# Gated graph layers: 1 - z from the sigmoid of the negated sum, and the state update as three GpSimd operations per half

## Chip, cores and metric

The kernel runs on one core of a Trainium2 chip. The metric is device time in microseconds (us) of one execution. Engines: TensorE (PE; PEld is its weight load), VectorE (DVE), ScalarE (ACT), GpSimd (POOL) and SyncE (SP).

## What is computed

Two graph networks follow each other, each with a residual and a layer norm. The change is in the first, four gated layers over 16 graphs of 1024 nodes with 128 channels:

```python
h = x
for i in range(4):
    hw = einsum('bnc,cd->bnd', h, weight[i])
    m = einsum('bjn,bjd->bnd', adj, hw)
    gx = m @ w_ih[i].T + b_ih[i];  gh = h @ w_hh[i].T + b_hh[i]
    xr, xz, xn = split(gx, 3);     hr, hz, hn = split(gh, 3)
    r = sigmoid(xr + hr)
    z = sigmoid(xz + hz)
    n = tanh(xn + r * hn)
    h = (1.0 - z) * n + z * h
x = layernorm(x + h * mask)
```

The second network thins the adjacency first (a sequential rule on rows and columns, `_dilate`), and then applies three graph convolutions with batch norm. The thinning needs only the adjacency, not the first network's output.

## The kernel before

The run has two parts. In the first, the class `Gated` computes the gated layers, and `FixPoint` the thinned adjacency beside it. In the second, `Sage` computes the convolutions. The change touches only `Gated`.

`Gated` holds two graphs at a time, as two streams. The loop in `run` goes over pairs of graphs, over the 4 layers, and over the two streams: 64 calls of `layer`. The state `h` of a graph lies transposed, channels on the 128 partitions and 1024 nodes along the row, and is worked on in two halves of 512 nodes (`f` = 0, 1). A call of `layer` has these parts:

- Aggregation (L1096): 32 matmuls, 8 blocks of the adjacency for the high and the low part of the split features, for both halves. The sums go through ACT to `h_ms` (L1099).
- Gates (L1108), for each half: r from two matmuls, the hidden and the input part of n from one each, z from two; each of these matmuls shows as two records. ACT makes r (L1118), DVE two operations on n's sum (L1121, L1123), ACT the tanh (L1124, into the tile `h_r`) and z (L1127, into `h_z`).
- Update: z*h (L1131 for half 0, L1135 for half 1) on POOL, (z - 1)*n on DVE (L1136), and new h = z*h - (z - 1)*n on POOL (L1137). For half 0 the first product stands right after z; the others stand after both halves. In the very last layer of the last graph, `aid` is DVE in place of POOL.

The order on all engines (PE, DVE, ACT, POOL, SP) is the order of the program's text, by a manual schedule: each engine takes its instructions in that order, and an instruction that waits holds back all behind it on its engine. What runs beside a layer is placed by calls of `aside(n)`, at fixed points of the layer. They do two things. They advance `FixPoint.steps` by one step (a scan of 128x1024 on DVE, L739; comparisons, L870, L872, L900; Abs on ACT; short transposes on PE; one affine_select on POOL, L780; loads of `f_a` on POOL's queue, L687). And they start the other stream's next layer: `next_layer` transposes that stream's h, half 0 at point 5, half 1 at point 7 (L1041), and splits it for the aggregation (L1029, L1034).

Between graphs there is a boundary layer, on each stream: `finish` transposes h back, masks it on ACT (L1071), adds it to x on POOL (L1074) and stores the sum from POOL's queue (L1076, `e_sum`); `load_x` loads the next graph's x (L1025), `load_adj` its adjacency (L1020), both from POOL's queue too; `begin_rows` splits the new x (ACT L1060, POOL L1061), `begin` transposes it (L1053). The x tiles have three buffers, so a load of x waits for the store of the graph three before it. The gate tiles `h_r`, `h_z`, `h_zh` have two buffers each, one for each half. L1992 on DVE looks over rows of the adjacency, once in each second layer.

Of the kernel before, what the change touches and what calls it, by code (L numbers as in the profile page):

```python
# [8 lines left out]
F32 = mybir.dt.float32  # L9
# [5 lines left out]
AF = mybir.ActivationFunctionType  # L15
ALU = mybir.AluOpType
# [8 lines left out]
C = 128  # L25
NB = N // P
HF = 512
L0 = 4
# [27 lines left out]
class Dilate:  # L56
# [15 lines left out]
    def __init__(self, ctx, tc, cst, adj, not_r):  # L72
        self.tc, self.nc, self.cst, self.adj, self.not_r = tc, tc.nc, cst, adj, not_r
        nc = self.nc
        pool = lambda name, **k: ctx.enter_context(tc.tile_pool(name=name, **k))
        self.one = pool("d_one", bufs=1)
        self.two = pool("d_two", bufs=2)
        self.small = pool("d_small", bufs=3)
        self.dram = pool("d_dram", bufs=1, space=DRAM)
        self.ps = pool("d_ps", bufs=1, space=PSUM)  # L80

        self.removed = [self.dram.tile([N, N], BF, name=f"rt{b}") for b in range(B)]

        self.coef = self.one.tile([B, ROW], F32, name="coef")  # L90
        nc.vector.memset(self.coef, 1.0)
        nc.vector.memset(self.coef[:, TAIL + 1:TAIL + 2], -1.0)
        nc.vector.memset(self.coef[:, TAIL + 2:TAIL + 3], -0.5)
        nc.vector.memset(self.coef[:, TAIL + 5:TAIL + 6], 2.0)
        self.stage = self.one.tile([P, B, ROW], BF, name="stage")
        for i, v in ((1, -8.5), (2, 1.0), (3, MAGIC), (4, -MAGIC), (5, 0.0)):
            nc.vector.memset(self.stage[:, :, TAIL + i:TAIL + i + 1], v)
        self.counts = self.one.tile([P, B, NB], F32, name="counts")
        self.free = {}
# [824 lines left out]
class Gated:  # L924
# [7 lines left out]
    def __init__(self, ctx, tc, cst, x, adj, weight, w_ih, w_hh, b_ih, b_hh, summed, bad):  # L932
        self.tc, self.nc, self.cst = tc, tc.nc, cst
        self.x, self.adj, self.summed, self.bad = x, adj, summed, bad
        nc = self.nc
        pool = lambda name, **k: ctx.enter_context(tc.tile_pool(name=name, **k))
        self.adjp = pool("h_adj", bufs=NB)
        self.one = pool("h_one", bufs=1)
        self.wk = pool("h_wk", bufs=2)

        self.ps6 = pool("h_ps6", bufs=6, space=PSUM)
        self.wi = self.one.tile([C, L0, 3, C], F32, name="h_wi")
        self.wh = self.one.tile([C, L0, 3, C], F32, name="h_wh")
        self.bi = self.one.tile([C, L0 * 3], F32, name="h_bi")
        self.bh = self.one.tile([C, L0 * 3], F32, name="h_bh")
        self.bs = self.one.tile([C, L0 * 3], F32, name="h_bs")
        self.given = weight, w_ih, w_hh, b_ih, b_hh

    def bank(self):
        return self.ps6.tile([P, HF], F32, name="h_g")  # L950
# [19 lines left out]
    def prepare(self):  # L970
        nc, ident = self.nc, self.cst["ident"]
        bank = self.bank
        three = lambda p: p[:, :3 * C].rearrange("p (g c) -> p g c", g=3)
        wt = self.wk.tile([P, 4, P], F32, name="h_w")
        for l in range(L0):
            for n, dst in enumerate((self.wi, self.wh)):
                pt = bank()
                for g in range(3):
                    nc.tensor.transpose(pt[:, g * C:(g + 1) * C], self.w_in[l, n][:, g, :], ident)
                (nc.vector.tensor_copy, nc.scalar.copy)[n](dst[:, l], three(pt))  # L980
            pt = bank()
            nc.tensor.transpose(pt[:, :C], self.w[:, l, :], ident)
            nc.vector.tensor_copy(wt[:, l, :], pt[:, :C])
        for l in range(L0):
            pt = bank()
            nc.tensor.matmul(three(pt), wt[:, l, :], self.wi[:, l], start=True, stop=True)
            (nc.vector.tensor_copy, nc.scalar.copy)[l % 2](self.wi[:, l], three(pt))

        for t, dst in zip(self.b_in, (self.bi, self.bh)):
            pt = bank()  # L990
            nc.tensor.transpose(pt[:, :L0 * 3], t, ident[:L0 * 3, :L0 * 3])
            nc.vector.tensor_copy(dst, pt[:, :L0 * 3])
        nc.vector.tensor_add(self.bs, self.bi, self.bh)

    def load_test(self, n):
        if n < B * 2:
            self.test = self.wk.tile([P, N], F32, name="h_test", bufs=1)
            self.nc.sync.dma_start(self.test, self.adj[n // 2, n % 2 * P:(n % 2 + 1) * P, :])
# [79 lines left out]
    def layer(self, st, l, aside):  # L1078

        nc, wk = self.nc, self.wk  # L1080

        aid = nc.vector if (st.b, l) == (B - 1, L0 - 1) else nc.gpsimd
        half = [slice(f * HF, (f + 1) * HF) for f in range(2)]
        bank = self.bank
        pm = [bank() for f in range(2)]
        ms = []
        for f in range(2):
            for n, part in enumerate((st.hi, st.lo)):
                if (f, n) != (0, 1):
                    aside(2 * f + n)  # L1090
                if l == 0 and f == 1 and n == 0:
                    st.begin(1)
                for j in range(NB):
                    if (f, n, j) == (0, 1, NB // 2):
                        aside(1)
                    nc.tensor.matmul(pm[f], part[:, j, :], st.adj[j][:, half[f]],  # L1096
                                     start=(j == 0 and n == 0), stop=(j == NB - 1 and n == 1))
            m = wk.tile([C, HF], F32, name="h_ms")
            nc.scalar.copy(m, pm[f])  # L1099
            ms.append(m)  # L1100
        aside(4)
        bias = lambda t, g: t[:, 3 * l + g:3 * l + g + 1]
        w = lambda t, g: t[:, l, g, :]

        def gate(*mm):
            pg = bank()
            for i, (lhs, rhs) in enumerate(mm):
                nc.tensor.matmul(pg, lhs, rhs, start=(i == 0), stop=(i == len(mm) - 1))  # L1108
            return pg

        rest = []
        for f in range(2):
            h, m = st.ht[:, half[f]], ms[f]
            r = wk.tile([C, HF], F32, name="h_r")
            z = wk.tile([C, HF], F32, name="h_z")
            zh = wk.tile([C, HF], F32, name="h_zh")
            pr = gate((w(self.wh, 0), h), (w(self.wi, 0), m))
            nc.scalar.activation(r, pr, AF.Sigmoid, bias=bias(self.bs, 0))  # L1118
            aside(5 + 2 * f)
            ph = gate((w(self.wh, 2), h))  # L1120
            nc.vector.scalar_tensor_tensor(r, ph, bias(self.bh, 2), r, op0=ALU.add, op1=ALU.mult)  # L1121
            px = gate((w(self.wi, 2), m))
            nc.vector.tensor_add(r, px, r)  # L1123
            nc.scalar.activation(r, r, AF.Tanh, bias=bias(self.bi, 2))  # L1124
            aside("rest" if f == 0 else 8)
            pz = gate((w(self.wh, 1), h), (w(self.wi, 1), m))
            nc.scalar.activation(z, pz, AF.Sigmoid, bias=bias(self.bs, 1))  # L1127

            rest.append((r, z, zh, h))
            if f == 0:  # L1130
                aid.tensor_tensor(zh, z, h, ALU.mult)  # L1131
                aside(6)
        for f, (r, z, zh, h) in enumerate(rest):
            if f == 1:
                aid.tensor_tensor(zh, z, h, ALU.mult)  # L1135
            nc.vector.scalar_tensor_tensor(r, z, 1.0, r, op0=ALU.subtract, op1=ALU.mult)  # L1136
            aid.tensor_tensor(h, zh, r, ALU.subtract)  # L1137
        aside(9)

    def run(self, steps):  # L1140
# [937 lines left out]
```

## Time and profile before

| | us |
|---|---|
| Runs | 2232.93, 2233.61, 2242.04; median 2233.61 |
| Profiled execution, its own time | 2232.83 |
| Its span in the profile | 2230.8 |
| Busy: PE, DVE, ACT, POOL | 2129.7, 1926.9, 1327.2, 1082.6 |
| Gated stage, first to last aggregation (L1096) | 34.0 to 1292.4 |
| Last gate matmul (L1108) | 1303.4 |

All times in the profile are from the start of the span. A row of the timeline gives the start, the length, the engine, the line, the operation, the tile written and those read with their shapes, and in brackets the idle time before and what ended it. A row of the groups gives the count, the busy time, the mean length in ns and the idle time before these instructions. Ends of matmuls are modelled, so the busy share of PE is to be read with the distances between its starts.

### The profile page before, as it was taken

The page shows a single profiled execution, that of the slowest core. Times are in us where ns is not written, and L with a number is a line of the kernel's source. Part 1 is how long each engine was busy: PE and PEld are TensorE (multiplying, and loading weights), DVE is VectorE, ACT ScalarE, POOL GpSimd, SP SyncE. Part 2 cuts the span into 40 slices and gives each one's busy share as a digit, 9 for nine tenths or more (in the row PEclk, how much of TensorE's full clock was granted, in tenths as well). Part 3 has the DMA queues.
Part 4 walks back from the last instruction along what each step waited for, and adds up shares of the span by engine and source line. Part 5 has one row for each costly group of instructions (what it writes and reads, how often), then busy time and mean ns, then how long its engine had stood idle before and what let it go on. Part 6 is the DMA issues. An engine that isn't in the chain of part 4 may idle for free. (4 is left out here: it accounts for less than half of the span.)

```text
span 2230.8 us, 33341 instructions
## 1 busy us (share of the span) xinstructions
PE 2129.7 (95%) x10665; PEld 1456.6 (65%) x10665; DVE 1926.9 (86%) x4338; ACT 1327.2 (59%) x3238; POOL 1082.6 (49%) x1092
## 2 busy tenths in 40 slices
PE   6999999999999999999999979999999899998987
PEld 4566655666656666555665557777777678887865
DVE  4999999999998999999999978888888766666877
ACT  3657557565565656556566465666666455556756
POOL 4347437356355364364463346777777344551002
PEclk9999999999999999999999989999999999999989
DMA  8247347347356265364383259888888577765404
GB/s 251 71 103 240 80 114 229 71 120 214 86 156 177 73 200 138 90 201 118 73 264 85 64 184 329 305 305 297 305 301 304 169 259 260 257 221 174 152 29 144
DMA packets 214396, 402.46 MB, mean 180 GB/s; under 512 B 59586, under 2 KB 80740, under 8 KB 214212
## 3 DMA queue, kind: packets, MB, share of 16 engines
q1 hardware_dynamic: 168388, 280.68, 37.3%
q0 software_dynamic: 41472, 117.46, 19.3%
q10 hardware_dynamic: 4352, 2.11, 0.4%
q8 instruction: 86, 1.41, 0.3%
q14 instruction: 98, 0.80, 0.1%
HBM read 324.49 MB, written 109.25 MB: 194 GB/s over the span
## 5 line engine op out<-in xcount | busy, mean ns | idle before, releaser
L1108 PE MATMUL h_g<-h_h,h_wh 128*128 128x512 f32 x768 | 399.2, 601 | 3.1 <-DVE h_r L1121 3.1
L1108 PE MATMUL h_g<-h_ms,h_wi 128*128 128x512 f32 x768 | 392.1, 592 | 0.0
L739 DVE TENSOR_TENSOR_SCAN f_rank<-f_a,f_first,f_pd 128x1024 f16<-128x1024 bf16 x128 | 299.2, 2343 | 3.3
L1137 POOL TENSOR_TENSOR h_h<-h_zh,h_r 128x512 f32<-128x512 f32 x126 | 205.3, 1629 | 195.2 <-DVE h_r L1136 172.2
L1096 PE MATMUL h_g<-h_a,h_hi 128*128 128x512 f32 x1024 | 282.8, 417 | 2.2 <-DMA h_a<-in_adj_dram 2.0
L1108 PEld LDWEIGHTS h_g<-h_ms,h_wi 128*128 128x128 f32 x768 | 145.6, 190 | 183.9 <-issue 166.8
L1096 PE MATMUL h_g<-h_a,h_lo 128*128 128x512 f32 x1024 | 264.1, 395 | 0.0
L1513 POOL CAST p_b<-p_at 128x512 uint8<-128x512 f32 x256 | 219.4, 879 | 84.2 <-DVE p_at L1505 59.8
L1096 PEld LDWEIGHTS h_g<-h_a,h_hi 128*128 128x128 f32 x1024 | 188.4, 188 | 63.8 <-issue 20.1
L1096 PEld LDWEIGHTS h_g<-h_a,h_lo 128*128 128x128 f32 x1024 | 190.0, 188 | 39.4
L1406 ACT ACTIVATE s_junk<-s_o 128x128 bf16<-128x128 f32 x384 | 114.0, 298 | 170.7 <-DVE s_o L1399 170.7
L1131 POOL TENSOR_TENSOR h_zh<-h_z,h_h 128x512 f32<-128x512 f32 x63 | 80.1, 1271 | 275.5 <-ACT h_z L1127 275.5
L1108 PEld LDWEIGHTS h_g<-h_h,h_wh 128*128 128x128 f32 x768 | 129.2, 190 | 85.9 <-issue 65.5
L1099 ACT COPY h_ms<-h_g 128x512 f32<-128x512 f32 x128 | 73.8, 577 | 183.3 <-PE h_g L1096 139.3
L1124 ACT ACTIVATE h_r<-h_r,h_bi 128x512 f32<-128x512 f32 x128 | 92.3, 721 | 131.2 <-DVE h_r L1123 131.1
L916 ACT ACTIVATE f_u<-f_rank,f_q 128x128 f16<-128x128 f16 (+7 forms) x128 | 110.6, 867 | 74.9 <-DVE f_rank L856 74.9
L1992 DVE SCALAR_TENSOR_TENSOR p_junk<-p_a 128x1024 bf16<-128x1024 f32 x96 | 125.7, 1309 | 0.0
L893 ACT ACTIVATE f_pd<-f_rank,f_q 128x128 f32<-128x128 f16 x128 | 59.1, 461 | 109.8 <-DVE f_q L701 106.6
L1781 PE MATMUL q_ob<-s_wxp,q_xt 128*128 128x256 f32 x512 | 123.4, 385 | 0.3
L1505 DVE SCALAR_TENSOR_TENSOR p_at<-p_nr,p_u 128x128 fp32r<-128x128 bf16 (+1 forms) x192 | 102.5, 543 | 20.5 <-ACT p_at L1497 15.0
L1492 PE MATMUL p_u<-ident_b,p_nr 128*128 128x128 bf16 x1024 | 97.2, 224 | 7.2 <-DVE p_at L1505 5.0
L1423 POOL TENSOR_TENSOR q_rl<-s_r,q_rh 128x512 fp32r<-128x512 f32 x32 | 41.1, 1285 | 128.0 <-ACT q_rh L1422 105.5
(260 smaller groups left out, 4946.3 us busy)
## 6 DMA issues: line engine op xcount, KB each, us to landing
h_a<-in_adj_dram POOLq DMA_DIRECT2D x128, 512.0 KB, 9.5
p_a<-in_adj_dram SPq DMA_DIRECT2D x96, 512.0 KB
f_a<-in_adj_dram POOLq DMA_DIRECT2D x128, 256.0 KB, 6.6
e_nr<-f_nr SPq DMA_DIRECT2D x128, 256.0 KB
p_nr<-e_nr SPq DMA_DIRECT2D x32, 1024.0 KB
h_test<-in_adj_dram SPq DMA_DIRECT2D x32, 512.0 KB
s_at<-p_b SPq DMA_DIRECT2D x32, 512.0 KB
s_ag<-s_ag SPq DMA_DIRECT2D x64, 256.0 KB
```

Of the source, the lines that this page charges most:

```text
L739: nc.vector.tensor_tensor_scan(out, a, other[:, 0, 0:1].to_broadcast([P, N]), start, op0=ALU.add, op1=ALU.bypass)
L916: nc.scalar.activation(u[:, :n1], rank[:, g, :n1], AF.Abs, bias=q[:, 1, g:g + 1], scale=q[:, 0, g:g + 1])
L1096: nc.tensor.matmul(pm[f], part[:, j, :], st.adj[j][:, half[f]], start=(j == 0 and n == 0), stop=(j == NB - 1 and n == 1))
L1108: nc.tensor.matmul(pg, lhs, rhs, start=(i == 0), stop=(i == len(mm) - 1))
L1124: nc.scalar.activation(r, r, AF.Tanh, bias=bias(self.bi, 2))
L1137: aid.tensor_tensor(h, zh, r, ALU.subtract)
L1406: self.nc.scalar.activation(junk, o[:, i, :], AF.Square, accum_out=ss[:, i:i + 1])
L1492: nc.tensor.matmul(pu[:, i * P:(i + 1) * P], v[:, 4 * f + i, j * P:(j + 1) * P], self.cst["ident_b"], start=True, stop=True)
L1505: self.nc.vector.scalar_tensor_tensor(g["at"][:, j, c0:c0 + low], v[:, j, c0:c0 + low], 0.0, pu[:, :low], op0=ALU.is_lt, op1=ALU.is_lt)
L1513: self.nc.gpsimd.tensor_copy(g["b", f][:, j, :], g["at"][:, j, f * HF:(f + 1) * HF].bitcast(F32))
L1781: nc.tensor.matmul(pb[:, i], g["xt"][:, f, blk], self.wxp, start=(i % 2 == 0), stop=False)
L1992: nc.vector.scalar_tensor_tensor(junk, a, 0.0, a, op0=ALU.is_gt, op1=ALU.not_equal, accum_out=bad[:, c:c + 1])
```

## The change

The bias of z's sigmoid is negated once (`h_bn`), and the sigmoid gets scale -1 with it, so the tile `h_z` holds 1 - z. The update is h + (1 - z)*(n - h): a subtraction, a product and a sum, all three on `aid`, that is on POOL except in the last layer. They follow z's sigmoid directly in each half. The product z*h, the DVE operation and the loop after both halves are gone.

```diff
@@ __init__ and prepare
+        self.bn = self.one.tile([C, L0 * 3], F32, name="h_bn")
...
         nc.vector.tensor_add(self.bs, self.bi, self.bh)
+        nc.vector.tensor_scalar(self.bn, self.bs, -1.0, None, op0=ALU.mult)
@@ layer
-        rest = []
         for f in range(2):
             h, m = st.ht[:, half[f]], ms[f]
             r = wk.tile([C, HF], F32, name="h_r")
             z = wk.tile([C, HF], F32, name="h_z")
-            zh = wk.tile([C, HF], F32, name="h_zh")
+            d = wk.tile([C, HF], F32, name="h_zh")
...
             pz = gate((w(self.wh, 1), h), (w(self.wi, 1), m))
-            nc.scalar.activation(z, pz, AF.Sigmoid, bias=bias(self.bs, 1))
-
-            rest.append((r, z, zh, h))
+            nc.scalar.activation(z, pz, AF.Sigmoid, bias=bias(self.bn, 1), scale=-1.0)
+            aid.tensor_tensor(d, r, h, ALU.subtract)
+            aid.tensor_tensor(d, z, d, ALU.mult)
+            aid.tensor_tensor(h, h, d, ALU.add)
             if f == 0:
-                aid.tensor_tensor(zh, z, h, ALU.mult)
                 aside(6)
-        for f, (r, z, zh, h) in enumerate(rest):
-            if f == 1:
-                aid.tensor_tensor(zh, z, h, ALU.mult)
-            nc.vector.scalar_tensor_tensor(r, z, 1.0, r, op0=ALU.subtract, op1=ALU.mult)
-            aid.tensor_tensor(h, zh, r, ALU.subtract)
         aside(9)
```

The order of the instructions in the two built programs, compared engine by engine: PE and SP have the same instructions in the same order. ACT differs in the operand of 128 sigmoids. DVE loses the two L1136 of each of 63 layers and gains the one for `h_bn`. POOL goes from 1760 to 1886 instructions, all 126 of them from the update.

The prediction calls the three new operations d, m and a, with the number of the half: d0 is n - h of half 0, m0 the product, a0 the sum; and those of before zh0, zh1 (z*h), stt0, stt1 (L1136), and h0, h1 (L1137).

## Prediction

> **What bounds the kernel now.** Only the first stage (the gated layers, with the dilation steps woven in) is edited, so I first cut the run into stretches, with the busy time of each engine. Columns: stretch, length, then busy us (and instructions) of PE, PE's weight loads, VectorE (DVE), ScalarE (ACT), GpSimd (POOL), granted clock, DMA share, GB/s.
>
> ```profile
> 59.00:1304.00 1245.00, 1238.55 (x4942) 751.46 (x4940) 1173.14 (x2360) 745.16 (x1390) 601.21 (x599) 1.00 0.47 135
> 1304.00:1318.00 14.00, 4.28 (x29) 3.31 (x29) 12.23 (x51) 6.95 (x18) 1.64 (x4) 0.66 1.04 388
> ```
>
> In the 1245 us of layers PE is idle for 6.45 us; DVE is at 94%, POOL at 48%. A busy PE need not be a PE at its rate, so I looked at starts in the timeline: the eight aggregation matmuls of 611.00 are followed by the next eight at 612.83 (229 ns each), and the gate matmuls of L1108, twelve a layer and each two records, follow each other at 0.86 us. Per layer that is 32 x 0.229 + 24 x 0.43 = 17.6 us, plus 8 transposes at 0.11 and some 13 short ones of the dilation at 0.055: 19.2 us, of the 19.8 that a layer takes (39.6 for a pair of layers). PE streams almost without holes, so the waits of PE show nearly all that an edit on other engines can win:
>
> ```profile
> PE h_g L1108 <- DVE h_r L1121: 3.1, 12, 0.3
> PE h_g L1096 <- DMA h_a<-in_adj_dram: 2.0, 4, 0.8
> PE h_g L1053 <- ACT h_z L1127: 0.8, 1, 0.8
> ```
>
> (total us, times, longest.) 5.9 us in 64 layers. The third view is the groups of the same stretch, for prices (count, busy us, mean ns, idle before):
>
> ```profile
> L1136 DVE SCALAR_TENSOR_TENSOR h_r<-h_z,h_r 128x512 f32<-128x512 f32 x124 | 96.5, 813 | 3.7 <-ACT h_z L1127 3.7
> L1137 POOL TENSOR_TENSOR h_h<-h_zh,h_r 128x512 f32<-128x512 f32 x125 | 203.7, 1630 | 192.2 <-DVE h_r L1136 169.2 <-PE f_pd L908 17.7
> L1135 POOL TENSOR_TENSOR h_zh<-h_z,h_h 128x512 f32<-128x512 f32 x62 | 80.0, 1291 | 0.0
> L1131 POOL TENSOR_TENSOR h_zh<-h_z,h_h 128x512 f32<-128x512 f32 x62 | 78.8, 1271 | 265.5 <-ACT h_z L1127 265.5
> ```
>
> POOL spent 192 us waiting for DVE's L1136; that wait disappears. Last, one layer's tail in the timeline (start, length):
>
> ```profile
> 605.63 1.27 POOL L1131 TENSOR_TENSOR h_zh<-h_z,h_h 128x512 f32<-128x512 f32 x1 [9.71 <-ACT h_z L1127]
> ...
> 608.38 0.71 ACT L1124 ACTIVATE h_r<-h_r,h_bi 128x512 f32<-128x512 f32 x1
> 609.00 0.67 ACT L1127 ACTIVATE h_z<-h_g,h_bs 128x512 f32<-128x512 f32 x1
> 609.52 1.28 DVE L1136 SCALAR_TENSOR_TENSOR h_r<-h_z,h_r 128x512 f32<-128x512 f32 x2
> ...
> 610.38 1.58 POOL L1137 TENSOR_TENSOR h_h<-h_zh,h_r 128x512 f32<-128x512 f32 x1 [3.47 <-DVE h_r L1136]
> 611.91 1.30 POOL L1135 TENSOR_TENSOR h_zh<-h_z,h_h 128x512 f32<-128x512 f32 x1
> ...
> 613.29 2.14 POOL L1137 TENSOR_TENSOR h_h<-h_zh,h_r 128x512 f32<-128x512 f32 x1
> ```
>
> The new h is finished at 611.96 (half 0) and 615.43 (half 1). PE first reads half 0 in the transposes of L1041 at 617.07, and half 1 at 622.66: 5 and 7 us of slack. The update is not on PE's path.
>
> **What the skill says.** "SBUF — State Buffer", section "Who interferes with whom": a DVE instruction in a two-port mode, or with two SBUF inputs, and a GpSimd instruction that reads SBUF shut each other out for a whole instruction. The trace agrees: L870, a DVE tensor_scalar, takes 0.48 us, but 1.50 from 614.23, while L1137 ran to 615.43 and itself took 2.14 instead of 1.29. "GPSIMD Engine Reference", section 3.1: elementwise work with two inputs is about twice as slow on GpSimd. Here 1.29 against 0.69 us (the same lines on DVE in the last layer): agrees. "ScalarE: Activation LUTs", "Step-by-step: what each stage is for": scale and bias are applied before the lookup in one operation, free. No run here has scale -1 on a sigmoid.
>
> **The change, part by part.**
>
> *Removed from DVE:* the L1136 group, 128 instructions, 99.1 us on the page; the last layer keeps its six elementwise operations per layer on DVE, so 126 go, about 97.7 us. DVE falls from 1173 to about 1075 us of 1245. None of this is on PE's path but for the 3.1 us in which PE waits for L1121, which stands behind a DVE backlog. I take 2 of the 3.1 as won (bounds 0 and 3.1).
>
> *Added to POOL:* 126 tensor_tensor of 128x512. Clean, one takes 1.29 us, disturbed on average 1.63. All 378 at 1.29 are 488 us against the present 362.5, so +125; at 1.63, +254. POOL goes from 601 to 726 (at most 855) of 1245: it stays free enough. I take 1.29, since the update moves away from L870: worked out below.
>
> *Moved:* the queue's order. Before: zh0, then (after half 1's DVE work) h0, zh1, h1. After: d0, m0, a0, then d1, m1, a1. The first operation now waits for tanh, which ends 0.6 us before the sigmoid of z, and nothing waits for DVE. In the layer above: half 0 from 605.0 to 608.9; d1 from 609.1 (tanh of half 1), m1 at 610.4, a1 to 613.0. Half 1 ends 2.4 us earlier than 615.43, although there are two more operations, and before the L870 at 614.23, so that DVE's 33 us of stretched L870, 128 x (737 - 480) ns, should shrink too. Off PE's path: costs and brings nothing directly. Without the slack of 5 us it would.
>
> *Queued behind it on POOL:* the loads of f_a (L687), h_a (L1020), h_x (L1025) and the store e_sum (L1076). Before the first boundary layer of each pair of graphs, the load of h_x and the four h_a loads follow directly on the tail (h1 ended at 973.65, the load of h_x started at 973.60). With a tail shorter by 2.4 us they start earlier. PE's waits for h_a at 351.79 (0.45), 669.48 (0.64) and 986.71 (0.16) are of these: 1.2 us won. In the boundary layer itself d0, m0, a0 stand before the store where zh0 alone did, so the store is issued 2 x 1.29 = 2.6 us later, and the next load of h_x waits for it:
>
> ```profile
> 986.79 0.60 POOL L1076 DMA_DIRECT2D e_sum<-h_x  x1 [0.30 <-POOL h_x L1074]
> ...
> 998.39 0.96 POOL L1025 DMA_DIRECT2D h_x<-in_x_dram  x1 [6.97 <-issue]
> ```
>
> The page names no releaser, but at the six other boundaries the same wait is put down to e_sum (22.8 us in all). What hides the 2.6: the store lies in the queue behind nine loads. The DMA share of the stretches around it:
>
> ```profile
> 987.00:992.00 5.00, 5.00 (x25) 4.10 (x25) 5.00 (x4) 1.07 (x2) 4.32 (x4) 1.00 1.11 410
> 992.00:995.00 3.00, 3.00 (x13) 1.78 (x12) 2.90 (x6) 0.59 (x1) 0.00 (x0) 1.00 0.65 251
> 995.00:998.40 3.40, 3.40 (x11) 1.69 (x10) 3.30 (x15) 3.08 (x8) 0.01 (x1) 1.00 0.01 4
> ```
>
> Counting the packets of POOL's DMA queue back from the last, the store's own begin 5.8 us after its issue here, and 5.0 to 6.0 at the other boundaries; an idle queue begins 1.6 us after issue. So 3.4 us of delay cost nothing; I take 0, bounds 0 and 2.6 each.
>
> *Edits of one answer:* scale -1 on 128 sigmoids, 0 (both bounds 0: L1127 at 671 ns has a pointer bias now too). The bn column, one DVE tensor_scalar of 128x12, about 0.17 us (the row of a 128x4 one) while the inputs still load: 0, or 0.17 uncovered.
>
> *The end:* the last layer's update lies on DVE and PE waits for it (3.1 and 1.4 us, L1041). After L1123 of half 1 there follow stt0, h0, zh1, stt1, h1; after the change d1, m1, a1, but three operations instead of one stand before half 1's L1121. Worked through, half 1 ends at 1308.4 instead of 1309.0: 0.6 won.
>
> **Sum.** 2 + 1.2 + 0.6 = 3.8 us, off 2232.83 of the profiled execution (span 2230.8 and 2.0 around it): 2229.0. The median of the runs, 2233.61, lies 0.8 above; I give 2229. Everything after 1318 us is untouched and taken as equal.
>
> **Rivals.** *Slower, the store is late.* If the added operations delay the store past the cover of 3.4 us, the next h_x and four h_a loads of seven boundaries slip, and PE, which waited there already at 1008.99 (0.76), slips with them. It decides at 1.7 us for each of the two added operations. Clean ones stay under it; at 2.14 they give 4.3, 0.9 over; if the cover is not there at all, 7 x 2.6 = 18 us: 2251. For it: PE's loads are nearly just in time. Against: the backlog. 12%. *Slower, port contention.* Each added operation shuts DVE out for its whole length: +163 us against -98, DVE at 1238 of 1245, and it becomes the bound, some 10 us late: 2243. Against: in the window where the new operations run (605 to 613) DVE mostly has one operand in PSUM. 7%. *Faster, DVE was a co-limiter.* PE wins all of its 6.45 us and the 5.8 us of waits in 1304 to 1318: 12 us, 2221. For it: DVE at 94%. Against: PE's spacing. 12%.
>
> **How the numbers follow.** No measurable change 69%, own range 2224 to 2236 (bounds of the wins, and the runs' spread). With the faster rival 81%: 2220 to 2241, which reaches into the milder part of contention. Half a per cent (11 us) is about what a measurement of this kernel tells from no change: faster 13%, same 69%, slower 18%.
>
> **What would show it.** PE idle in the layers still 3 to 6 us; DVE near 1060 to 1080 us, POOL near 730; the d, m, a lines at 1.29 us; no POOL wait for DVE's h_r; h_x loaded 7 to 12 us after the store, not later. It is wrong if PE's waits for h_a or h_x grow, if the new lines take over 1.7 us, or if the time after the layers moves.

## The result, and the profile after

| | before | after |
|---|---|---|
| Median of runs, us | 2237.22 (5 runs: the three above and two more, 2232.93 to 2242.04) | 2223.35 (5 runs, 2220.9 to 2226.26) |
| Profiled execution (span), us | 2232.83 (2230.8) | 2226.26 (2224.5) |
| First to last gate matmul, start to start, us | 1261.5 (41.89 to 1303.41) | 1250.9 (42.65 to 1293.53) |

The ratio is 0.9946, with a 95% interval of 0.9934 to 0.9957: about 12 us faster (10 to 15), where 4 were forecast. The time lies inside the range of 2220 to 2241, but 0.65 us beyond the edge of "no change", 2224. The two terms for the layers had the right causes and were two to four times too small.

The two profiled executions differ by 6.3 us, less than the layers, because the second part, which the change does not touch, took 922.7 us in after and 919.2 in before; 2.6 of these 3.5 us were lost around a stretch of 6.8 us near 2043 us that has half the granted clock. The next view gives three stretches of after, the last of them with this drop; columns as in the prediction (length, busy PE, PEld, DVE, ACT, POOL, then clock, DMA share and GB/s).

```profile
59.00:1304.00 1245.00, 1236.12 (x4964) 755.41 (x4963) 1097.86 (x2267) 751.88 (x1403) 727.43 (x726) 1.00 0.48 138
...
1304.00:1318.00 14.00, 9.75 (x71) 7.90 (x69) 8.60 (x31) 9.89 (x23) 9.11 (x14) 0.62 0.41 152
...
2040.00:2050.00 10.00, 6.97 (x31) 5.48 (x29) 5.87 (x17) 6.07 (x28) 0.00 (x0) 0.67 0.32 109
```

POOL is up by 126 us, as computed (+125). DVE is down by 75, but the stretch now holds 8.6 us of what follows the layers; from the first to the last gate matmul it is down by 85 (1185.7 to 1100.7), where the forecast was 98. The clock drop isn't the change's: a second profile of each kernel has 3.4 us of it near 2050 us, before and after alike, and there the spans are 2233.7 and 2225.7.

All that PE still waits for in the layers (from 59 to 1294 us; total, times, longest):

```profile
PE h_g L1110 <- DVE h_r L1122: 0.8, 4, 0.2
PE h_g L1098 <- DMA h_a<-in_adj_dram: 0.3, 1, 0.3
PE h_g L1055 <- ACT h_z L1128: 0.2, 1, 0.2
PE f_tr L726 <- DVE f_nr L872: 0.2, 1, 0.2
```

The list fell from 5.9 to 1.5 us, so it accounts for 4.4 us. The starts of PE's work moved by more, which is taken up below. The groups of POOL and DVE of after (59 to 1290 us; count, busy, mean ns, idle before), POOL first:

```profile
L1131 POOL TENSOR_TENSOR h_h<-h_h,h_zh 128x512 f32<-128x512 f32 x125 | 166.7, 1334 | 9.8
L1129 POOL TENSOR_TENSOR h_zh<-h_r,h_h 128x512 f32<-128x512 f32 x124 | 160.8, 1297 | 296.3 <-ACT h_r L1125 293.1
L1130 POOL TENSOR_TENSOR h_zh<-h_z,h_zh 128x512 f32<-128x512 f32 x124 | 159.7, 1288 | 9.7
```

And two of DVE's dilation steps in the same view:

```profile
L872 DVE TENSOR_TENSOR f_nr<-f_w,f_a 128x1024 bf16<-128x1024 bf16 x128 | 95.3, 745 | 4.4
...
L870 DVE TENSOR_SCALAR f_w<-f_u,f_q 128x1024 bf16<-128x1024 f16 x128 | 80.1, 626 | 17.2 <-ACT f_u L919 17.1
```

The three operations run at 1.29 to 1.33 us; nothing on POOL waits for DVE's h_r. L870 fell from 737 to 626 ns on average, L872 rose from 693 to 745. The layer of the prediction, in POOL's timeline of after:

```profile
602.10 1.26 POOL L1129 TENSOR_TENSOR h_zh<-h_r,h_h 128x512 f32<-128x512 f32 x1 [10.91 <-ACT h_r L1125]
...
604.80 1.30 POOL L1131 TENSOR_TENSOR h_h<-h_h,h_zh 128x512 f32<-128x512 f32 x1
606.22 1.29 POOL L1129 TENSOR_TENSOR h_zh<-h_r,h_h 128x512 f32<-128x512 f32 x1
...
608.96 1.29 POOL L1131 TENSOR_TENSOR h_h<-h_h,h_zh 128x512 f32<-128x512 f32 x1
```

The update runs as it was worked out, in two blocks of 4.0 us, with the whole layer some 3 us earlier. DVE's next L870, at 611.26, now takes 0.48 us; what meets the update there is one L1988 (L1992 of before) with 2.13 us (1.64 before).

**Where the time went.** The distances between the starts of the aggregation, one layer to the next, can be compared pair by pair. Sums over the 63 distances, in us against the first profile of before, for all kernels run (l is the layer from 0, s the stream; the columns: first layers of the later seven pairs of graphs on stream 0, where the boundary's loads must be there; the same on stream 1; layers 1 to 3 on stream 0 of the second, fourth, sixth and eighth pair, 12 layers, here "odd pairs"; the other 37):

| Kernel | all | l0, s0 | l0, s1 | odd pairs | rest | median of runs - before |
|---|---|---|---|---|---|---|
| after | -10.6 | -3.8 | -1.2 | -3.8 | -1.8 | -13.9 |
| after, again | -9.9 | -4.1 | -0.2 | -3.8 | -1.8 | -10.6 |
| before, again | +0.4 | -0.6 | +1.1 | 0.0 | 0.0 | +0.9 |
| e1: old operations, early | +50.8 | -4.1 | +9.8 | +9.5 | +35.6 | +52.6 |
| e2: spare two-input operation | +71.7 | -1.9 | +5.5 | +32.3 | +35.8 | +75.0 |
| e3: update late | +18.3 | +14.5 | +0.1 | -3.4 | +7.1 | +17.7 |
| e4: store later | -8.3 | -3.6 | +0.8 | -3.6 | -1.9 | -8.2 |
| e5: spare one-input operation | -6.6 | -4.4 | -1.4 | +0.3 | -1.2 | -7.3 |
| e7: last half 0 on POOL | -10.6 | -3.8 | -1.2 | -3.8 | -1.8 | -11.0 |

(e1 to e4 against 11 runs of before, median 2234.37; the others against 29, 2235.41; after against its own five.) The gain has two main parts of about the same size: the boundaries (the two l0 columns), and the odd pairs. (The other 37 layers give 0.05 us each; I didn't trace these.) My theory after the result was that the first comes from POOL's earlier queue, which starts the loads sooner, and the second from the operation taken off DVE. The rival was that one of them alone brings all of it.

### The profile page after: what moved, and what is told of

It is laid out like the page before. It is cut to its first block, busy times and chain, and to the rows that moved or that the text cites. A ratio compares the mean times of both kernels' runs of the same rounds, so it can differ in the third digit from the quotient of the medians.

```text
span 2224.5 us, 33612 instructions
## 1 busy us (share of the span) xinstructions
PE 2127.9 (96%) x10665; PEld 1460.0 (66%) x10665; DVE 1841.0 (83%) x4213; ACT 1328.5 (60%) x3238; POOL 1210.6 (54%) x1218
## 5 line engine op out<-in xcount | busy, mean ns | idle before, releaser
L1129 POOL TENSOR_TENSOR h_zh<-h_r,h_h 128x512 f32<-128x512 f32 x126 | 163.4, 1297 | 307.1 <-ACT h_r L1125 303.9
L1131 POOL TENSOR_TENSOR h_h<-h_h,h_zh 128x512 f32<-128x512 f32 x126 | 168.0, 1334 | 9.9
L1130 POOL TENSOR_TENSOR h_zh<-h_z,h_zh 128x512 f32<-128x512 f32 x126 | 162.3, 1288 | 9.9
L1988 DVE SCALAR_TENSOR_TENSOR p_junk<-p_a 128x1024 bf16<-128x1024 f32 x96 | 125.6, 1309 | 0.0
```

Source lines behind the costliest of these rows:

```text
L1129: aid.tensor_tensor(d, r, h, ALU.subtract)
L1130: aid.tensor_tensor(d, z, d, ALU.mult)
L1131: aid.tensor_tensor(h, h, d, ALU.add)
L1988: nc.vector.scalar_tensor_tensor(junk, a, 0.0, a, op0=ALU.is_gt, op1=ALU.not_equal, accum_out=bad[:, c:c + 1])
```

## Experiments

**e1_early_order_dve_kept.** The old three operations, but in the new place: POOL's queue is early, DVE keeps its work. Against before:

```diff
+            aid.tensor_tensor(zh, z, h, ALU.mult)
+            nc.vector.scalar_tensor_tensor(r, z, 1.0, r, op0=ALU.subtract, op1=ALU.mult)
+            aid.tensor_tensor(h, zh, r, ALU.subtract)
             if f == 0:
-                aid.tensor_tensor(zh, z, h, ALU.mult)
                 aside(6)
-        for f, (r, z, zh, h) in enumerate(rest): ...
```

> The old three operations (z*h and the difference on GpSimd, (z-1)*n on DVE) put at the new place, right after z in each half; DVE keeps its 126 operations. Theory (the 10.6 us won in the layers come in about equal parts from DVE stalls of PE that are gone and from GpSimd's queue being earlier at the graph boundaries): ratio to before about 0.998, and PE's waits for L1121 stay. Rival A (only DVE's relief counts): 1.000. Rival B (only the earlier place in the queue counts): 0.995, like the changed kernel.

Measured: 2286.97 us, ratio 1.0231 (1.0213 to 1.0248). The expectation failed. DVE's group of this operation in e1, from 59 to 1290 us:

```profile
L1129 DVE SCALAR_TENSOR_TENSOR h_r<-h_z,h_r 128x512 f32<-128x512 f32 x118 | 89.5, 759 | 80.7 <-ACT h_z L1126 80.5
```

The largest entry of PE's waits in e1, over the same stretch:

```profile
PE f_pd L908 <- DVE f_x L900: 28.2, 27, 3.4
```

The operation did not get longer (759 ns, 813 in before), but DVE now stands 80.5 us waiting for the sigmoid of z, and PE waits for the dilation's L900 that is queued some operations behind it. The boundary's first layer won its 4 us all the same (-4.1), though its loads also had more time, since the layer before it (layer 3 on stream 1) is 1.2 to 1.8 us longer here. So the early place is open only because no DVE operation stands there any more; what it is worth to POOL, e3 and e5 tell better.

**e2_dve_load_back.** After, with DVE's old work done again as spare work where it stood (nothing is left out):

```diff
+            pairs.append((z, r))
...
+        for z, r in pairs:
+            spare = wk.tile([C, HF], F32, name="h_spare", bufs=1)
+            nc.vector.scalar_tensor_tensor(spare, z, 1.0, r, op0=ALU.subtract, op1=ALU.mult)
         aside(9)
```

> The changed kernel with two spare DVE operations of the old kind per layer, (z-1)*n into a spare tile, at their old place behind both halves; nobody waits for them, GpSimd's new order stays. Theory: the stalls for DVE come back, some 4 to 6 us of the 10.6, those of the boundaries do not: ratio 0.997. Rival A (only DVE's relief counts): 1.000. Rival B (only GpSimd's place counts): 0.995.

Measured: 2309.36 us, ratio 1.0332 (1.0315 to 1.0348). Failed too, for a reason that the edit brought in. DVE's group of the spare operation in e2:

```profile
L1138 DVE SCALAR_TENSOR_TENSOR h_spare<-h_z,h_r 128x512 f32<-128x512 f32 x116 | 159.4, 1374 | 9.1 <-ACT h_z L1129 3.8
```

One pair of them in the timeline of e2, with POOL's update:

```profile
642.65 1.29 POOL L1130 TENSOR_TENSOR h_zh<-h_r,h_h 128x512 f32<-128x512 f32 x1
643.00 3.18 DVE L1138 SCALAR_TENSOR_TENSOR h_spare<-h_z,h_r 128x512 f32<-128x512 f32 x2
...
644.02 1.61 POOL L1131 TENSOR_TENSOR h_zh<-h_z,h_zh 128x512 f32<-128x512 f32 x1
...
645.72 1.62 POOL L1132 TENSOR_TENSOR h_h<-h_h,h_zh 128x512 f32<-128x512 f32 x1
```

The same operation took 813 ns before and takes 1374 here: the two of DVE and the three of POOL meet, and both sides stretch (POOL's L1131 and L1132 take 1468 and 1446 ns on average). That is the contention of the prediction's rival "port contention", at full size. e2 therefore can't say what DVE's relief is worth.

**e5_dve_load_one_input** asks the same with an operation that reads one SBUF tile:

```diff
-            nc.vector.scalar_tensor_tensor(spare, z, 1.0, r, op0=ALU.subtract, op1=ALU.mult)
+            spare = wk.tile([C, 1], F32, name="h_spare")
+            nc.vector.tensor_reduce(spare, r, axis=AX.X, op=ALU.max)
```

> The changed kernel with a spare DVE reduction of each half's tile r (one SBUF input, so it should not shut GpSimd out; estimated 0.6 us, 126 of them some 75 us) at the place of the old DVE operation. This puts DVE's load back without the mutual blocking that lengthened the spare operation of the run before from 0.68 to 1.37 us. Theory now: the gain of the ordinary layers (5.6 of the 10.6 us) is DVE's relief, that of the boundary layers (5.0 us) is GpSimd's earlier queue; so 4 to 7 us over the changed kernel, ratio to before 0.997, the first boundary layer of each pair stays at its new length. Rival (DVE itself is the bound as soon as anything is added): 40 us or more over, ratio 1.015. Rival (all of the gain is the queue): as the changed kernel, 0.995.

Measured: 2228.11 us, ratio 0.9967 (0.9956 to 0.9978), 3.3 us over the median of after's second set of runs (2224.82); layers 4.0 us longer than in after's first profile, 3.3 than in its second, at or just under the lower edge of what was expected. DVE's group of the spare operation in e5:

```profile
L1138 DVE TENSOR_REDUCE h_spare<-h_r 128x1 f32<-128x512 f32 x124 | 79.3, 678 | 0.6 <-ACT h_r L1126 0.6
```

PE's waits in the layers of e5:

```profile
PE h_g L1110 <- DVE h_r L1123: 3.3, 12, 0.3
PE f_tr L726 <- DVE f_nr L872: 0.4, 1, 0.4
```

The 12 waits of PE for the first DVE operation on n's sum are back, with 3.3 us in place of before's 3.1, one in each of the twelve layers of the odd pairs, as in before. The odd pairs lost all their gain (+0.3 against before), the boundaries kept theirs (-4.4). POOL's three operations kept their lengths (1.29 to 1.30 us on average). (The reduction needs only n and not z as well; in e2 DVE waited 3.8 us in all for z, so that is a small part of what tells the two runs apart.) The times of the runs barely tell this kernel from after, but the sums of the odd pairs repeat to 0.1 us between profiles of one kernel. This is the run that separates the two halves of the gain, and both parts of the theory hold.

**e3_update_deferred.** The new operations, none on DVE, but products and sums behind both halves, as the old loop had it:

```diff
             aid.tensor_tensor(d, r, h, ALU.subtract)
-            aid.tensor_tensor(d, z, d, ALU.mult)
-            aid.tensor_tensor(h, h, d, ALU.add)
+            late.append((z, d, h))
...
+        for z, d, h in late:
+            aid.tensor_tensor(d, z, d, ALU.mult)
+            aid.tensor_tensor(h, h, d, ALU.add)
         aside(9)
```

> The changed kernel with only the subtraction right after z; product and sum of both halves behind the second half, as the old update stood. DVE is relieved as in the change; GpSimd's tail ends about 2.6 us later in ordinary layers, but the store of the finished graph is issued 2.6 us earlier. Theory: ratio 0.995 to 0.996: the boundary part moves by 1 to 2 us one way or the other, the part of the ordinary layers stays. Rival A: 0.995. Rival B (the earlier place in the queue counts): 0.998 or more.

Measured: 2252.05 us, ratio 1.0073 (1.0058 to 1.0089): slower than before, where a gain was expected. PE's waits in the layers of e3:

```profile
PE h_g L1098 <- DMA h_a<-in_adj_dram: 12.5, 10, 2.7
PE f_tr L726 <- DVE f_nr L872: 6.6, 24, 0.6
```

POOL's timeline ahead of the third pair's first load, in before, in after and in e3:

```profile
336.29 2.14 POOL L1137 TENSOR_TENSOR h_h<-h_zh,h_r 128x512 f32<-128x512 f32 x1
338.38 0.97 POOL L1025 DMA_DIRECT2D h_x<-in_x_dram  x1
```

```profile
334.22 2.19 POOL L1131 TENSOR_TENSOR h_h<-h_h,h_zh 128x512 f32<-128x512 f32 x1
336.35 0.97 POOL L1027 DMA_DIRECT2D h_x<-in_x_dram  x1
```

```profile
337.40 2.28 POOL L1136 TENSOR_TENSOR h_h<-h_h,h_zh 128x512 f32<-128x512 f32 x1
339.65 1.46 POOL L1135 TENSOR_TENSOR h_zh<-h_z,h_zh 128x512 f32<-128x512 f32 x1
341.18 1.60 POOL L1136 TENSOR_TENSOR h_h<-h_h,h_zh 128x512 f32<-128x512 f32 x1
342.73 0.97 POOL L1027 DMA_DIRECT2D h_x<-in_x_dram  x1
```

In e3 five operations stand behind the last tanh, and they run into L870 and L872 (820 and 930 ns on average). The load of h_x is issued 10.6 us after the start of that layer's aggregation; in before it was 8.8, in after 7.4. The l0, s0 layers of e3 take 14.5 us more, and the odd pairs keep their -3.4. The other 37 layers lose 7.1; most of PE's 6.6 us of waits for the stretched L872 lie there. An edit of POOL's order alone, with the stretching that it brings, separates a gain of 4 us in these boundary layers from a loss of 14.

**e4_store_later** tests the prediction's rival of the late store: two more POOL operations of 1.29 us ahead of the store, at seven boundaries (spare work):

```diff
+            if f == 0 and l == L0 - 1 and st.s == 1 and st.b < B - 1:
+                for _ in range(2):
+                    spare = wk.tile([C, HF], F32, name="h_spare", bufs=1)
+                    nc.gpsimd.tensor_tensor(spare, z, r, ALU.mult)
```

> The changed kernel with two spare GpSimd operations (2 x 1.29 us) behind half 0's update in seven layers only, those ahead of the store at a graph boundary. In the changed kernel the next load of x follows 4.6 us after the store at four of the seven boundaries, the shortest distance seen, so the cover is used up. Theory: the load slips by 2.6 us at these boundaries and PE by part of it: 3 to 10 us over the changed kernel, ratio 0.996 to 0.999. Rival (still hidden): as the changed kernel, 0.995. The full price would be 18 us.

Measured: 2226.17 us, ratio 0.9961 (0.9947 to 0.9976); layers 2.3 us longer than in after's first profile and 1.6 than in its second, under the 3 to 10 that were expected. Against after the load of h_x slipped in its layer by 2.5 to 3.4 us at four of the seven boundaries and by 0.3 to 0.7 at the other three, 12.6 us in all. PE's waits for h_a in e4:

```profile
PE h_g L1098 <- DMA h_a<-in_adj_dram: 1.1, 3, 0.5
```

So PE lost at most a fifth of what the loads slipped, and the boundary layers vary by about 1 us without any change. With the 1.7 to 2.4 us by which after already issues the store later, the rival's point of 3.4 us is passed here; it doesn't decide at the point that I gave it.

**e7_last_half_on_pool.** In the last layer, half 0's update goes to POOL, with half 1's left on DVE:

```diff
-        aid = nc.vector if (st.b, l) == (B - 1, L0 - 1) else nc.gpsimd
...
+            aid = nc.vector if (st.b, l, f) == (B - 1, L0 - 1, 1) else nc.gpsimd
```

> The changed kernel, but in the last layer half 0's three operations run on GpSimd (idle there), and only half 1's on DVE. In the changed kernel half 1's first DVE step starts at 1294.73, behind three update operations and the last steps of the dilation, though its matmul had run at 1292.9; PE then waits 4.87 us for the last half. Expected: that wait shrinks to about 3.1 us, 1 to 2 us under the changed kernel; the ratio of runs will not resolve it (0.994), the trace will. Rival (GpSimd is too slow there and half 0 becomes late): the wait grows by 1 us.

Measured: 2224.42 us, ratio 0.9952 (0.9939 to 0.9966). The stage's last transposes, in PE's timeline of after:

```profile
1299.43 1.08 PE L1043 MATMUL h_g<-ident,h_h 128*128 128x128 f32 x4 [4.87 <-DVE h_h L1131]
```

The same in e7:

```profile
1298.02 0.63 PE L1043 MATMUL h_g<-ident,h_h 128*128 128x128 f32 x4 [2.85 <-DVE h_h L1131]
```

From the last gate matmul to the first matmul of the second part it is 6.1 us in place of 8.3. That is 2.2 us in the trace, of which 1.7 are left at that part's third group of matmuls. The runs can't resolve it: their median is 0.4 us below that of after's second set (2224.82).

**before_again and after_again** are the two kernels once more, beside e5 and e7, for the table's spread:

> The kernel before, a second profile: 1.000. If the layers are fixed by the program, the first to the last gate matmul take 1261.5 us again within 0.5; what differs between runs then lies after them.

> The changed kernel, a second profile: ratio 0.995, first to last gate matmul 1250.9 us within 0.5. The clock drop at 2043 us in the first profile, which that of the kernel before lacks, comes back only if it belongs to the change; I expect it to be chance.

Measured: 2236.3 us, ratio 1.0002 (0.9994 to 1.001), and 2224.82 us, ratio 0.9948 (0.9935 to 0.9961). First to last gate matmul is 1261.9 us, as expected, and 1251.6, which misses the 1250.9 by 0.7 where 0.5 was allowed; 1.0 us of it lies in one boundary layer. The odd pairs and the rest repeat to 0.1 us; the boundary layers vary by about 1 us between profiles of one kernel, so their -3.8 is known to about that. Of the 11.5 us between these two medians, the layers hold 10.2 (-9.9 against +0.4); the last 1 or 2 us are within the spread of the runs and are not traced.

## Why the prediction was right, and where its sizes were off

**The number.** The forecast gain was 3.8 us, the layers won 10.6, and the medians differ by 13.9. That 2229 came within 6 us of the measured time is in part luck: the median of before turned out at 2237.22, and 3.8 off that would have been 2233.4, 10 us too slow. The time lies in the range only because the range had been widened for the faster rival. Three of my own signs did not come: PE's idle time up to 1293.5 us is 1.8 us and not 3 to 6, DVE stays above 1080 us, and the load of h_x follows 4.6 to 8.2 us after the store and not 7 to 12.

**The waits as a limit: the step that failed.** I took PE's list of waits, 5.9 us, as nearly all that an edit elsewhere can win. The layers won 10.6. My own working had shown the gap: 19.2 us of counted PE work in a layer of 19.8 leaves 0.6 x 64 = 38 us, of which the list names 5.9. Here is a piece of an odd pair's layer in PE's timeline of before:

```profile
324.19 1.02 PE L1108 MATMUL h_g<-h_ms,h_wi 128*128 128x512 f32 x2
325.27 0.63 PE L1041 MATMUL h_g<-ident,h_h 128*128 128x128 f32 x4
325.80 0.38 PE L908 MATMUL f_pd<-f_tri,f_x 128*128 128x128 bf16 x4
326.46 1.12 PE L1108 MATMUL h_g<-h_h,h_wh 128*128 128x512 f32 x2 [0.28 <-DVE h_r L1121]
```

The same piece in after:

```profile
323.89 1.02 PE L1110 MATMUL h_g<-h_ms,h_wi 128*128 128x512 f32 x2
324.74 0.60 PE L1043 MATMUL h_g<-ident,h_h 128*128 128x128 f32 x4
325.18 0.39 PE L908 MATMUL f_pd<-f_tri,f_x 128*128 128x128 bf16 x4
325.77 1.13 PE L1110 MATMUL h_g<-h_h,h_wh 128*128 128x512 f32 x2 [0.21 <-DVE h_r L1122]
```

The listed wait shrank by 0.07 us. From the first start to the last it is 2.27 us before and 1.88 after: 0.39 won. In before the transposes start 1.08 us after the pair of gate matmuls instead of 0.85, and no idle time is shown, because the modelled end of the pair (1.02 us) covers nearly all of it. The Trainium skill warns of this row: "Trainium Kernel Development and Optimization", section "Performance Expectations", calls matmul busy time a bad metric for how close a kernel is to its roofline, because matmuls are pipelined. The trace agrees (0.39 us won, 0.07 of it listed), and I had even written that a busy PE need not be at its rate; I then used the idle time of the same row as a limit.

**DVE waits, 2 of 3.1 us won.** Right in kind. The list fell by 2.3 us (3.1 to 0.8), the distances of the odd pairs, where all these waits lie, by 3.8. e5 shows that DVE's load is the cause.

**Boundary loads, 1.2 us won.** Right in kind, a quarter to a third of the size: -3.8 on stream 0 and -1.2 (in the second profile -0.2) on stream 1. e3 shows that POOL's place in the order is the cause, with DVE relieved as in after, and e5 that DVE's relief is not needed for it; e1 agrees. PE's wait for h_a fell from 2.0 to 0.3.

**The store, delay hidden.** Right in its effect: the store is issued 1.7 to 2.4 us later in its layer than before, and yet the next load of h_x is issued 0.7 to 1.6 us earlier. The load was to follow 7 to 12 us after the store; it is 6.1 to 8.2 us at three of the seven boundaries and 4.6 at the other four. POOL's timeline of after, at one of the four:

```profile
193.39 0.60 POOL L1078 DMA_DIRECT2D e_sum<-h_x  x1 [0.30 <-POOL h_x L1076]
194.01 1.31 POOL L1129 TENSOR_TENSOR h_zh<-h_r,h_h 128x512 f32<-128x512 f32 x1
195.40 1.29 POOL L1130 TENSOR_TENSOR h_zh<-h_z,h_zh 128x512 f32<-128x512 f32 x1
196.77 1.29 POOL L1131 TENSOR_TENSOR h_h<-h_h,h_zh 128x512 f32<-128x512 f32 x1
198.00 0.97 POOL L1027 DMA_DIRECT2D h_x<-in_x_dram  x1
```

Nothing waits for the store here: its issue and the three operations of half 1 fill the 4.6 us without idle time. In before POOL stood idle for 2.9 to 3.5 us ahead of these four loads. The store itself lands 3.3 to 3.5 us after its issue at these four, in place of 7.2 to 7.9. That the loads queued ahead of it were issued sooner would explain this; no run tests it alone. So the cover was not used up, as the expectation of e4 took it to be.

**The end, 0.6 us won.** Wrong where it was priced: 8.3 us to the next stage's first matmul in place of 8.1 (its third group of matmuls is 0.3 us ahead). L1129 of half 0 took 1.18 us on DVE and L900 x4 took 2.18, each beside an operation of POOL, then DVE's L1122 of half 1 began only at 1294.73. Three operations ahead of it on a busy DVE are what e7 takes away.

**POOL's added work and scale -1, nothing.** Right: 1.29 to 1.33 us an operation, and the sigmoid at 673 ns on average where it was 671.

**The rivals.** The faster one (2221, 12%) named one of the two causes, DVE as a co-limiter, but priced it by the same idle time, and 5.8 us of it at the end, where next to nothing was won. Its number came out nearer to the measured 2223.35 than mine, but by other terms, which is luck. Contention at the price that I gave it didn't come: the new place mostly avoids DVE's two-input operations, and POOL's took 1.29 to 1.33 us on average. e2 shows what it costs where it isn't avoided: +75 us on before, where the rival had priced it at 10.

## What to carry to other kernels

Take the limit of a gain from distances between starts on the bounding engine, layer against layer, not from its listed idle time. Ask of an operation moved early in an in-order queue what it waits for there: the same place that let POOL's loads start sooner cost 50 us while one DVE operation stood in it. If a change moves work to an engine whose operations stretch together with those of the first, as those of POOL and DVE do in e2, price what meets in time, not the sum of busy times.

## What the hardware showed unexpectedly

DVE and POOL operations with two SBUF inputs stretched each other, and not only the one that came second: in e2 the spare operation on DVE took 1.37 us on average (0.81 for the same operation in before), and the two POOL operations beside it 1.47 and 1.45 (1.29 and 1.33 in after). "SBUF — State Buffer", section "Who interferes with whom", says that on this chip a reduction never contends with GpSimd; e5 agrees, in that 126 of them at 0.68 us cost 4 us in all, where the two-input operation cost 82 us over after's layers. A second surprise is that a store that is issued about 2 us later can land earlier: 3.3 to 3.5 us from issue to landing in place of 7.2 to 7.9 at four boundaries (after and before).
